# The order of the convolution's parts on TensorE, and a first radial layer of 128 rows, in a two-layer graph network

## The chip, the cores and the metric

The kernel runs on one core of a Trainium2 chip. The metric is the device time of one execution in microseconds, lower is better. A run's time is that of the slowest core, which here is the only one. The core has five engines that run their own instruction queues in order: PE (TensorE, matrix products, with its weight loads shown as PEld), DVE (VectorE), ACT (ScalarE), POOL (GpSimd) and SP (SyncE), and 16 DMA engines. Engines wait for each other by semaphores.

## The reference

There are 6250 nodes with 128 features, and 206,250 directed edges sorted by destination (100,000 random pairs in both directions and one loop per node). Two layers follow each other, each with a residual and a layer norm.

```
# layer 0: attention over incoming edges, then layer norm, a 128-512-128 network, layer norm
m      = leaky_relu(xl[src] + xr[dst] + edge_attr_128 @ W_e)
logits = einsum(m, att);  alpha = softmax over the edges of one dst
out    = segment_sum(xl[src] * alpha, dst)
...
# layer 1: a convolution over incoming edges
h   = gelu(edge_attr_8 @ W_mlp1 / sqrt(8));  h = gelu(h @ W_mlp2 / 8)
w00, w01, w10, w11 = h @ Wp_00, h @ Wp_01, h @ Wp_10, h @ Wp_11
e0, e1 = feat0[src], feat1[src]                 # 32 scalars and 32 vectors of a node
mid0 = concat(w00 * e0 * ea0,  w11 * sum(e1 * ea1))
mid1 = concat(w01 * e0 * ea1,  w10 * e1 * ea0)
n0, n1 = segment_sum(mid0, dst), segment_sum(mid1, dst)
y = cos * self + sin * (n0 @ W2_0e, n1 @ W2_1o)
```

All of it is computed in float32. The node features `feat` that the convolution gathers by source are the output of layer 0, so the convolution's first gather needs the last node of layer 0.

## The kernel before

Edges are cut into tiles of 128, one edge per partition, and into units of 6 tiles (768 edges): 269 units. The class `Fast` runs, in this order, `prologue`, `tables`, `attention` and `convolution`. Rows of a table in DRAM are fetched by source node with one indirect DMA per tile, issued by POOL in `gather` (line 365): 24 in the tables, 1590 in the attention (`xl<-fXL`), and 1614 in the convolution (`f<-fFEAT`).

The convolution, which is where the change lies, goes over 135 pairs of units, each in three parts (`PARTS`) of 2 x 2 tiles. These are its steps for a pair `p` and a part `c`:

- `load(p)` (L766, L768): SP loads the pair's 8 edge scalars, transposed, as a tile `e8` of 16 rows (8 for each unit) by 768, and the 4 edge attributes as `e4`. The pool `ld` gives three buffers for `e8` and four for `e4`.
- `fetch(p)`: POOL issues 12 gathers into a tile `f`, of which there are four.
- `radial(p, k)` (L783, L784): PE multiplies by `m1` (16 x 128) for k = 0 or `m2` (128 x 128, block diagonal) for k = 1, in two halves of 384 columns, and ACT applies the gelu. The result `h1` holds the hidden layer of the two units, 64 rows each.
- `filters(p, c)` (L790): two matmuls give the filter values `w` of four tiles in PSUM. There are three buffers of `w`, one for each part.
- `products(p, c)` (L799, L805, L810, L814): DVE builds a one-hot of the local destination, multiplies it by the edge attributes (`os`), and multiplies `w` by the gathered features (`vy`). There are two buffers each of `os` and `vy`.
- `sums(p, c)` (L831, L833): PE adds up the four tiles by eight matmuls with `vy` as the stationary operand and `os` as the moving one, into `y` in PSUM (two buffers).
- `collect(p)` (L841): DVE adds `y` to the accumulator `acc` at the unit's first destination.
- `nodes.step` runs one further step of `finish`, which takes two finished blocks of 128 nodes through the last product (L889), the layer norm and the store (L901).

In the trace a float32 matmul is two records of PE and two of PEld. The order on each engine is written out by hand (`manual_schedule`) by the loop at the end of `convolution`; the compiler's planner merges the stages where they meet. The indices `p + 2` in that loop are loads, gathers and radials two pairs ahead.

Of the kernel before, what the change touches and what calls it, by code (L numbers as in the profile page):

```python
# [8 lines left out]
F32 = mybir.dt.float32  # L9
# [7 lines left out]
P = 128  # L17
# [18 lines left out]
UE = TU * P  # L36
# [7 lines left out]
HEAD = (3, 4)  # L44
RAW = 4
ENDING = 28


def fast_sizes(n_nodes, n_edges):
# [57 lines left out]
class Fast:  # L107
# [628 lines left out]
    def convolution(self):  # L736


        tc, nc, a, NU = self.tc, self.nc, self.a, self.NU
        NPR, CT = -(-NU // 2), 2  # L740
        PARTS = TU // CT
        with ExitStack() as st:
            def pool(n, b, **k):
                return st.enter_context(tc.tile_pool(name=n, bufs=b, **k))
            cw, ld, wk = pool("fcw", 1), pool("fcl", 3), pool("fck", 2)
# [4 lines left out]
            for x in range(0, self.NX, step):  # L750
                nc.vector.memset(acc[:, :, x:min(x + step, self.NX)], 0.0)
            nodes = Queue(self.finish(st, yp, acc), self.done)
            m1 = cw.tile([16, P], F32, name="m1")
            nc.scalar.dma_start(m1, a["m1"])
            m2 = cw.tile([P, P], F32, name="m2")
            nc.scalar.dma_start(m2, a["m2"])
            wq = cw.tile([P, 2 * D], F32, name="wq")
            nc.scalar.dma_start(wq, a["wq"])
            fs, e8s, e4s, hs, h1s, ws, vys, ys = {}, {}, {}, {}, {}, {}, {}, {}

            def units(p):
                return min(2, NU - 2 * p)

            def load(p):
                e8s[p] = ld.tile([16, UE], F32, name="e8")
                nc.sync.dma_start(e8s[p], a["e8t"][p])  # L766
                e4s[p] = ld.tile([P, 2 * TU, 4], F32, name="e4", bufs=4)
                nc.sync.dma_start(e4s[p], a["e4t"][:, p * 2 * TU:(p + 1) * 2 * TU, :])  # L768

# [5 lines left out]

            def radial(p, k):

                m, x, sc = (m1, e8s, 1.0 / math.sqrt(8.0)) if k == 0 else (m2, h1s, 1.0 / 8.0)
                x = x.pop(p)
                h = (h1s, hs)[k][p] = wk.tile([P, UE], F32, name=f"h{k}")  # L780
                for s in (slice(0, UE // 2), slice(UE // 2, UE)):
                    ps = hp.tile([P, UE // 2], F32, name="h_ps")
                    nc.tensor.matmul(ps, m, x[:, s], start=True, stop=True)  # L783
                    nc.scalar.activation(h[:, s], ps, AF.Gelu_apprx_tanh, scale=sc)  # L784

            def filters(p, c):
                w = ws[p, c] = wp.tile([P, 2 * CT, D], F32, name="w")
                for t in range(CT):
                    e = (c * CT + t) * P
                    nc.tensor.matmul(w[:, 2 * t:2 * t + 2, :], hs[p][:, e:e + P], wq, start=True, stop=True)  # L790
# [29 lines left out]
            def sums(p, c):  # L820


                m = units(p)
                os, vy = vys.pop((p, c))
                if c == 0:
                    ys[p] = yp.tile([P, 2, 4, W], F32, name="y", bufs=2)
                for t in range(CT):
                    for i in range(m):
                        e = 2 * t + i
                        last = c == PARTS - 1 and t == CT - 1 and i == m - 1  # L830
                        nc.tensor.matmul(ys[p][:, i, 0], vy[:, e, 0], os[:, e, 3],  # L831
                                         start=(c == t == i == 0), stop=False)
                        nc.tensor.matmul(ys[p][:, i, 1:], vy[:, e, 1], os[:, e, :3], start=False, stop=last)  # L833

            def collect(p):
                y = ys.pop(p)
                for i in range(units(p)):
                    u = 2 * p + i
                    r = nc.vector.value_load(self.r0[0:1, u:u + 1], min_val=0, max_val=self.n)  # L839
                    v = acc[:, :, bass.ds(r, W)]  # L840
                    nc.vector.tensor_add(v, v, y[:, i])  # L841

            for p in range(min(2, NPR)):
# [1 line left out]
                fetch(p)  # L845
                radial(p, 0)
                radial(p, 1)
            for c in range(PARTS):
                filters(0, c)
            for p in range(NPR + 1):  # L850
                if p + 2 < NPR:
                    load(p + 2)
                    fetch(p + 2)
                for c in range(PARTS):
                    if p < NPR:
                        products(p, c)
                    if p + 1 < NPR:
                        filters(p + 1, c)
                    if c == 1 and p:
                        collect(p - 1)  # L860
                    if p < NPR:
                        sums(p, c)
                    if c != 1 and p + 2 < NPR:
                        radial(p + 2, c // 2)
                    if p:
                        nodes.step(min(2 * p, NU) - 1)
            nodes.rest()


# [548 lines left out]
def _fast_layout(a, g, q):  # L1418
    import numpy as np

    f = np.float32
    n, e = a["x"].shape[0], a["src"].shape[0]
    NU, UP, NP = fast_sizes(n, e)
    EP = NU * UE

    def padded(v, size, fill):
        return np.concatenate([v, np.full((size - len(v),) + v.shape[1:], fill, v.dtype)])

    dst = padded(a["dst"], EP, n)

    more = np.repeat(np.arange(n + 1, n + 1 + UP - NU), UE).astype(dst.dtype)
    dstf = np.concatenate([np.full(1, -1, dst.dtype), dst, more, np.full(1, 2 * n + UP, dst.dtype)])
    x = padded(a["x"], NP, 0)
    ea = padded(a["edge_attr_128"], EP, 0).reshape(NU, UE, D).transpose(0, 2, 1)
    pairs = -(-NU // 2)
    e8 = padded(a["edge_attr_8"], pairs * 2 * UE, 0).reshape(pairs, 2, UE, 8)
    e8 = e8.transpose(0, 1, 3, 2).reshape(pairs, 16, UE)
    e4 = padded(a["edge_attr_4"], pairs * 2 * UE, 0).reshape(pairs, 2, TU, P, 4).transpose(3, 0, 2, 1, 4)
    e4 = e4.reshape(P, -1, 4)[:, :, [1, 2, 3, 0]]

    p = np.arange(P)
    k = np.arange(R8)

    def same(r, c):
        m = np.zeros((P, len(c)), f)
        m[:len(r)] = r[:, None] == c[None]
        return m

    consts = np.concatenate([
        same(p, p),  # L1450
        np.tile(np.arange(W, dtype=f), (P, 1)),
        same(p % W, np.arange(W)),
        same(k % H, p // O),
        same(k + H, k),
        -same(k, k), same(k // H, np.arange(U)),
        same(p, np.arange(H) * O),
        (p % W)[:, None].astype(f)], axis=1)

    u = np.arange(32)
    outer = [u] + [32 + u * 3 + i for i in range(3)]  # L1460
    inner = [c * 32 + u for c in range(4)]
    wfs = np.zeros((D, 2 * D), f)
    w2ab = np.zeros((D, 4, D), f)
    for c in range(4):
        w1 = q["W1_0e"] if c == 0 else q["W1_1o"]
        wfs[np.ix_(outer[c], inner[c])] = w1[:, :32]
        wfs[np.ix_(outer[c], D + outer[c])] = w1[:, 32:]
        w2 = q["W2_0e"] if c == 0 else q["W2_1o"]
        first, second = (w2[:32], w2[32:]) if c == 0 else (w2[32:], w2[:32])
        w2ab[inner[c][:, None], 0, outer[c][None]] = first  # L1470
        for k in (range(1, 4) if c == 0 else [c]):
            w2ab[inner[k if c == 0 else 0][:, None], k, outer[c][None]] = second
    m1 = np.zeros((16, P), f)
    m2 = np.zeros((P, P), f)
    for i in range(2):
        m1[i * 8:i * 8 + 8, i * 64:i * 64 + 64] = q["W_mlp1"]
        m2[i * 64:i * 64 + 64, i * 64:i * 64 + 64] = q["W_mlp2"]
    wq = np.zeros((P, 2 * D), f)
    for i in range(2):
        wq[i * 64:i * 64 + 64, i * D:(i + 1) * D] = np.concatenate(  # L1480
            [q["Wp_00"], q["Wp_01"], q["Wp_10"], q["Wp_11"]], axis=1)
    arrays = {
        "consts": consts,
        "r0": dst[::UE][None],
        "need": np.array(fast_plan(n, e)[2], np.int32)[None],
        "dstf": dstf[None],
        "srct": padded(a["src"], EP, 0).reshape(-1, P).T,
        "dstt": dst.reshape(-1, P).T,
        "x": x,
        "xt": x.T,  # L1490
        "eat": ea,
        "e8t": e8,
        "e4t": e4,
        "w3": np.stack([g["W_l"], g["W_r"], g["W_e"]], axis=1),
        "b_lr": np.concatenate([g["b_l"], g["b_r"]])[None],
        "att": g["att"].reshape(1, -1),
        "rows": np.stack([g[k] for k in ("b_att", "g1", "be1", "b2", "g2", "be2")]),
        "w1": g["W1"],
        "b1": g["b1"].reshape(-1, P).T,
        "w2": g["W2"],  # L1500
        "wfs": wfs,
        "w2ab": w2ab,
        "m1": m1,
        "m2": m2,
        "wq": wq,
    }
    return {k: np.ascontiguousarray(v) for k, v in arrays.items()}
# [105 lines left out]
```

## Time and profile before

| | |
|---|---|
| median of 3 runs | 4443.35 us (4433.61 to 4454.99) |
| profiled execution | 5630.61 us, span 5628.8 us |
| granted TensorE clock, mean of the span | 0.713 |
| attention's gathers (first to last) | 59 to 2673 us |
| first gather of the convolution | 2840.5 us |
| last gather of the convolution | 5564.6 us |
| gathers of the attention / of the convolution | 1590, mean 1067 ns / 1614, mean 955 ns |
| filters L790 | 1620 records, 645.5 us busy |
| sums L831 and L833 | 3228 records each, 667.1 and 918.9 us busy |
| first radial matmuls (16 rows) / second (128 rows) | 540 records, 249.4 us / 540 records, 323.1 us |

A row of the groups gives the line, the engine, the operation, its output and inputs, the count, busy time and mean duration, and then the idle time of the engine just before, with what ended most of it. "issue" is time in which the engine waited for nothing that the profile shows, "remote" is a wait whose releaser isn't told. PEclk is the granted TensorE clock, as a part of full speed. Rows of the order in time start with the start and the duration in microseconds; idle time before is in brackets.

### The profile page before, as it was taken

Reading aid. Unit: us, or ns where it says so; the run is one execution under the profiler, and the core shown is the slowest. Engines: PE = TensorE matmul, PEld = TensorE weight load, DVE = VectorE, ACT = ScalarE, POOL = GpSimd, SP = SyncE. Lnnn points to the kernel's source line nnn. Section 1 sums busy time; section 2 is a strip of 40 time slices with the busy share of each in tenths; the row PEclk is TensorE's granted clock in tenths of the full one; section 3 lists DMA queues with packets and bytes.
Section 4 is the critical chain, followed back from the end, with each engine's and each line's share of the span. In section 5 each row is a group of like instructions: output and inputs, shape, how many; then the busy total and the mean of one; then the engine's idle time right before and its main releaser. Section 6 shows DMA issues by size and latency. Waiting matters only on the chain. (4 is left out here: it accounts for less than half of the span.)

```text
span 5628.8 us, 67318 instructions
## 1 busy us (share of the span) xinstructions
PE 4052.6 (72%) x21381; PEld 3207.9 (57%) x21381; DVE 2536.3 (45%) x5657; ACT 947.9 (17%) x2530; POOL 3262.0 (58%) x3232
## 2 busy tenths in 40 slices
PE   3666666676666676665648778788887888778878
PEld 2454555555545555544536666676666666667656
DVE  1455655655655665554713333333333333333333
ACT  1111222222221222211311111111111111111111
POOL 6256666766766766765045555555555555555553
PEclk6577777777777777767756766676767766666766
DMA  4443444444443444433111111111111111111111
GB/s 117 133 111 108 113 108 111 116 108 112 112 113 107 117 112 111 109 103 99 35 40 44 45 47 43 44 46 47 47 46 45 47 47 45 47 41 47 44 43 28
DMA packets 292393, 427.71 MB, mean 76 GB/s; under 512 B 124589, under 2 KB 201359, under 8 KB 292031
## 3 DMA queue, kind: packets, MB, share of 16 engines
q0 software_dynamic: 103296, 218.27, 16.0%
q1 hardware_dynamic: 185146, 197.75, 11.7%
q10 hardware_dynamic: 3588, 7.31, 0.4%
q8 instruction: 174, 2.85, 0.2%
q14 instruction: 189, 1.54, 0.1%
HBM read 403.04 MB, written 19.96 MB: 75 GB/s over the span
## 5 line engine op out<-in xcount | busy, mean ns | idle before, releaser
L365 POOL DMA_INDIRECT f<-fFEAT,fsrc x1614 | 1542.0, 955 | 1349.3 <-DVE oh L799 597.0
L365 POOL DMA_INDIRECT xl<-fXL,fsrc x1590 | 1696.9, 1067 | 934.5 <-issue 429.2
L790 PE MATMUL w<-wq,h 128*128 128x256 f32 x1620 | 645.5, 539 | 470.3 <-DVE vy L814 259.4
L805 DVE TENSOR_TENSOR os<-oh,e 128x512 f32<-128x512 f32 x405 | 280.6, 693 | 1490.4 <-remote 581.9
L833 PE MATMUL y<-os,vy 128*128 128x96 f32 x3228 | 918.9, 375 | 34.5 <-issue 34.4
L790 PEld LDWEIGHTS w<-wq,h 128*128 128x128 f32 x1620 | 396.0, 265 | 717.8 <-issue 395.7
L419 PE MATMUL z<-fw,ea 128*128 128x136 f32 x3228 | 654.8, 347 | 142.1 <-DVE pr L438 66.4
L831 PEld LDWEIGHTS y<-os,vy 128*128 128x128 f32 x3228 | 714.7, 258 | 73.0 <-issue 23.3
L833 PEld LDWEIGHTS y<-os,vy 128*128 128x128 f32 x3228 | 670.4, 256 | 35.6 <-issue 35.5
L831 PE MATMUL y<-os,vy 128*128 128x32 f32 x3228 | 667.1, 293 | 28.0 <-issue 26.6
L419 PEld LDWEIGHTS z<-fw,ea 128*128 128x128 f32 x3228 | 554.6, 242 | 208.0 <-issue 106.4
L784 ACT ACTIVATE h<-h_ps 128x384 f32<-128x384 f32 x540 | 252.8, 489 | 2418.5 <-remote 823.9
L528 PE MATMUL m<-xl,oh 128*32 128x136 f32 x3228 | 247.5, 348 | 239.6 <-ACT s L511 92.7
L814 DVE TENSOR_TENSOR vy<-w,f 128x384 f32<-128x384 f32 (+1 forms) x810 | 408.0, 545 | 0.0
L541 PEld LDWEIGHTS m<-fcst,sb 128*128 128x128 f32 x1076 | 191.2, 234 | 359.0 <-ACT sb L533 199.5
L541 PE MATMUL m<-fcst,sb 128*128 128x32 f32 x1076 | 180.3, 299 | 228.6 <-ACT sb L533 166.8
L783 PE MATMUL h_ps<-h,m 128*128 128x384 f32 x540 | 323.1, 738 | 23.5 <-issue 22.9
L422 PE MATMUL z<-xl,fcst 128*128 128x408 f32 x538 | 310.9, 660 | 15.4 <-issue 15.0
L528 PEld LDWEIGHTS m<-xl,oh 128*32 128x32 f32 x3228 | 128.7, 126 | 297.5 <-ACT s L511 95.1
L444 DVE TENSOR_REDUCE lg<-pr 128x48 f32<-128x816 f32 x269 | 266.8, 992 | 1.6 <-DVE pr L438 1.6
L519 DVE TENSOR_TENSOR xl<-xl,ex 128x768 f32<-128x768 f32 x269 | 255.3, 949 | 15.6 <-ACT ex L504 15.6
L419 PE MATMUL z<-xr,oht 96*128 96x136 bf16 x1614 | 227.5, 254 | 39.8 <-issue 34.2
(143 smaller groups left out, 4130.3 us busy)
## 6 DMA issues: line engine op xcount, KB each, us to landing
ea<-fast_eat_dram SPq DMA_DIRECT2D x269, 384.0 KB
lb<-fLB SPq DMA_DIRECT2D x269, 144.0 KB
f<-fFEAT,fsrc POOLq DMA_INDIRECT x1614
xl<-fXL,fsrc POOLq DMA_INDIRECT x1590
xr<-fXR SPq DMA_DIRECT2D x807, 8.5 KB
e<-fast_e8t_dram SPq DMA_DIRECT2D x135, 48.0 KB
fXR<-pt SPq DMA_DIRECT2D x16, 306.0 KB
fXL<-tb SPq DMA_DIRECT2D x16, 204.0 KB
```

What stands on the lines that cost most here:

```text
L365: self.nc.gpsimd.indirect_dma_start(out=to, out_offset=None, in_=table, in_offset=bass.IndirectOffsetOnAxis(ap=self.src[:, g:g + 1], axis=0))
L419: nc.tensor.matmul(z[:, t * ZW:(t + 1) * ZW], lhs[:, e], rhs, start=(t == 0 and lhs is ea), stop=(half == 1 and t == 2 and lhs is oht))
L422: nc.tensor.matmul(z, self.ident, xl[:, :3, :].rearrange("p t f -> p (t f)"), start=False, stop=True)
L444: nc.vector.tensor_reduce(lgs[b][:, :, i * H:(i + 1) * H], prs.pop(u).rearrange("p (t h) o -> p t h o", h=H), axis=mybir.AxisListType.X, o ...
L528: nc.tensor.matmul(ag[q * W:(q + 1) * W], oh[:, t, :], xl[:, t, :], start=(t < 4), stop=(t + 4 >= TU))
L541: nc.tensor.matmul(nd[:, i, j], sb[:, j], self.s4, start=True, stop=True)
L783: nc.tensor.matmul(ps, m, x[:, s], start=True, stop=True)
L790: nc.tensor.matmul(w[:, 2 * t:2 * t + 2, :], hs[p][:, e:e + P], wq, start=True, stop=True)
L805: nc.vector.tensor_mul(os[:, own], oh.rearrange("p t u w -> p (t u) w")[:, own, None, :].to_broadcast([P, n, 4, W]), e4s[p][:, at, :, None ...
L814: nc.vector.tensor_mul(vy[:, own, j, 32:].rearrange("p t (c x) -> p t c x", c=3), w[:, :, None, 64 + j * 32:96 + j * 32].to_broadcast([P, ...
L831: nc.tensor.matmul(ys[p][:, i, 0], vy[:, e, 0], os[:, e, 3], start=(c == t == i == 0), stop=False)
L833: nc.tensor.matmul(ys[p][:, i, 1:], vy[:, e, 1], os[:, e, :3], start=False, stop=last)
```

## The change

Three things are changed, all in `convolution` and the arrays that it loads.

The loop runs over parts `q = 3 p + c` instead of pairs and parts. At part `q` it issues products(q), then collect of the pair before (at c = 1), then sums of part q - 1, then filters of part q + 2, then the radial (at c = 0 and 2), then the step of the nodes. Before, a part was products(q), filters(q + 3), collect, sums(q), radial, nodes. Ahead of the loop there are now two filters instead of three.

The first radial layer works on 128 rows: one tile `e8` holds eight pairs one below the other (16 rows each), loaded at once, with two buffers. `m1` becomes eight matrices of 128 x 128, of which matrix k has the weights in rows 16 k to 16 k + 15 and zeros elsewhere, so that the product picks out pair k of the eight. The last group has seven pairs and 112 rows.

The constant `EB = 8` is that number of pairs.

```diff
-            m1 = cw.tile([16, P], F32, name="m1")
+            m1 = cw.tile([P, EB, P], F32, name="m1")
             nc.scalar.dma_start(m1, a["m1"])
...
             def load(p):
-                e8s[p] = ld.tile([16, UE], F32, name="e8")
-                nc.sync.dma_start(e8s[p], a["e8t"][p])
+                if p % EB == 0:
+                    g = min(EB, NPR - p)
+                    e8 = ld.tile([P, UE], F32, name="e8", bufs=2)
+                    nc.sync.dma_start(e8[:g * 16], a["e8t"][p:p + g].rearrange("g k e -> (g k) e"))
+                    for i in range(g):
+                        e8s[p + i] = e8[:g * 16], m1[:g * 16, i]
...
-                m, x, sc = (m1, e8s, 1.0 / math.sqrt(8.0)) if k == 0 else (m2, h1s, 1.0 / 8.0)
-                x = x.pop(p)
+                if k == 0:
+                    (x, m), sc = e8s.pop(p), 1.0 / math.sqrt(8.0)
+                else:
+                    x, m, sc = h1s.pop(p), m2, 1.0 / 8.0
...
-            for c in range(PARTS):
-                filters(0, c)
-            for p in range(NPR + 1):
-                if p + 2 < NPR:
+            for q in range(2):
+                filters(q // PARTS, q % PARTS)
+
+            for q in range(NQ + PARTS):
+                p, c = q // PARTS, q % PARTS
+                if c == 0 and p + 2 < NPR:
                     load(p + 2)
                     fetch(p + 2)
-                for c in range(PARTS):
-                    if p < NPR:
-                        products(p, c)
-                    if p + 1 < NPR:
-                        filters(p + 1, c)
-                    if c == 1 and p:
-                        collect(p - 1)
-                    if p < NPR:
-                        sums(p, c)
-                    if c != 1 and p + 2 < NPR:
-                        radial(p + 2, c // 2)
-                    if p:
-                        nodes.step(min(2 * p, NU) - 1)
+                if q < NQ:
+                    products(p, c)
+                if c == 1 and p:
+                    collect(p - 1)
+                if 0 < q <= NQ:
+                    sums((q - 1) // PARTS, (q - 1) % PARTS)
+                if q + 2 < NQ:
+                    filters((q + 2) // PARTS, (q + 2) % PARTS)
+                if c != 1 and p + 2 < NPR:
+                    radial(p + 2, c // 2)
+                if p:
+                    nodes.step(min(2 * p, NU) - 1)
...
-    m1 = np.zeros((16, P), f)
+    m1 = np.zeros((P, EB, P), f)
...
+        for k in range(EB):
+            m1[k * 16 + i * 8:k * 16 + i * 8 + 8, k, i * 64:i * 64 + 64] = q["W_mlp1"]
```

## The prediction

> **What bounds the kernel now.** I read the page first (busy times, slices), then the groups by line, the waits of the last stage, and PE and POOL in order of time with busy times by stretch.
>
> ```profile
> span 5628.8 us, 67318 instructions
> PE 4052.6 (72%) x21381; PEld 3207.9 (57%) x21381; DVE 2536.3 (45%) x5657; ACT 947.9 (17%) x2530; POOL 3262.0 (58%) x3232
> POOL 6256666766766766765045555555555555555553
> PEclk6577777777777777767756766676767766666766
> ...
> L365 POOL DMA_INDIRECT f<-fFEAT,fsrc x1614 | 1542.0, 955 | 1349.3 <-DVE oh L799 597.0
> L365 POOL DMA_INDIRECT xl<-fXL,fsrc x1590 | 1696.9, 1067 | 934.5 <-issue 429.2
> ```
>
> No engine is full, TensorE's clock is granted at 0.7, and POOL, which only gathers rows, has idle time that DVE ends. Taken alone this page says: PE and DVE hold each other up, POOL has room. But the page is of an execution of 5630.61 us (1.8 us around its span), and the median of the runs is 4443.35, 21% less. The extra must sit somewhere. PE in order of time, at the start of the convolution, shows where:
>
> ```profile
> 2882.26 0.21 PE L831 MATMUL y<-os,vy 128*128 128x32 f32 x1 [1.88 <-issue]
> 2885.06 0.32 PE L833 MATMUL y<-os,vy 128*128 128x96 f32 x1 [2.59 <-issue]
> 2887.86 0.32 PE L833 MATMUL y<-os,vy 128*128 128x96 f32 x1 [2.48 <-issue]
> ```
>
> One small matmul every 2.8 us, waiting for nothing that is shown; elsewhere a whole part's sixteen such records take 1.75 (3671.45 to 3673.20). Such stretches recur. I take them to belong to the profiled execution (inferred: only something of this size explains the 21%). POOL keeps its pace in the same stretch:
>
> ```profile
> 2840.54 0.94 POOL L365 DMA_INDIRECT f<-fFEAT,fsrc  x1 [166.28 <-DMA fBASE<-h]
> 2841.79 0.94 POOL L365 DMA_INDIRECT f<-fFEAT,fsrc  x1 [0.30 <-issue]
> ```
>
> 1.249 us from gather to gather (0.94 + 0.30) wherever nothing blocks it. So for the median I build the time from POOL. Head until the first xl gather 59; attention 1590 x (1.067 + 0.30) = 2174; pause until the first f gather, 167 in the profile, of which I estimate 40 to be PE's backlog and stalls: 127; convolution 1614 x 1.249 = 2016; tail after the last gather, 63 profiled, some 25 to 30 when PE is not two pairs behind. Sum 4401 to 4406. With everything as profiled it is 59 + 2174 + 167 + 2016 + 63 = 4479, with undisturbed gathers in attention (1590 x 1.249 = 1986) and the short pause and tail 4213. The measured 4443 lies inside, so gathers alone nearly fill the median: some 40 us are left over, for both stages (0 to 230 by the ends).
>
> Now the convolution per pair of units. POOL: 12 x 1.249 = 15.0 us. DVE, from the groups: 3 x (0.28 + 0.69 + 0.42 + 2 x 0.55) + 2 x 0.28 = 8.0. PE depends on its clock:
>
> ```profile
> core 0: us, PE busy (x) PEld busy (x) DVE busy (x) ACT busy (x) POOL busy (x), PEclk, DMA share, GB/s
> 3602.00:3609.00 7.00, 7.00 (x23) 5.04 (x22) 2.15 (x5) 0.78 (x2) 0.92 (x1) 0.50 0.02 4
> 3630.00:3638.00 8.00, 8.00 (x32) 7.28 (x32) 2.15 (x5) 0.14 (x1) 5.97 (x6) 0.51 0.20 55
> 3666.00:3680.00 14.00, 12.95 (x84) 10.84 (x84) 8.02 (x23) 1.49 (x4) 7.98 (x8) 1.00 0.14 39
> 3000.00:5500.00 2500.00, 2028.56 (x8709) 1640.95 (x8710) 888.01 (x2256) 315.32 (x606) 1403.69 (x1471) 0.70 0.17 45
> ```
>
> PE is busy without a gap at clock 0.50 in the first two rows, at 1.00 in the third. In order of time, a pair at full clock runs from 3666.18 to 3679.12, less 1.82 of output matmuls (L889): 11.1 us. At half clock its pieces are filters 1.87, sums 3.36, radial 2.85 (16 rows) and 2.57: 3 x 5.23 + 5.42 = 21.1. PE keeps up with POOL's 15.0 if it does over (21.1 - 15.0) / 10.0 = 61% of its work at full clock.
>
> **The Trainium skill.** "TensorE: Matmul & The Clock Gate", Part 1, says that the clock is halved or full by how busy PE was in windows of about 3.4 us. The trace agrees on 0.50 and 1.00, and adds that full occupancy doesn't suffice: the first two rows hold a first radial layer (16 rows) or mostly weight loads with small matmuls, and stay at half; the clock rises at the ends of pairs, around the second layer (128 rows). The same page, "LDWEIGHTS", says that a load costs by columns, not rows; shortest records here are 181 (16 rows) against 186 ns (128), and 481 against 486 for the matmuls: agrees. "Perfetto Trace Analysis", "DMA Instruction — SWDGE (GPSIMD)", says the record of such a DMA ends when its descriptors are made: so 0.94 us is POOL's own work, which the 1.249 pace bears out, and no faster consumer shortens it.
>
> **The change part by part.**
> (1) Order on PE. Before, a step is filters(q+3), sums(q), radial; the filters wait until products(q) has read the buffer, and the first filters of a pair follow at once on the radial that feeds them, through ACT:
>
> ```profile
> PE w L790 <- DVE vy L814: 216.7, 68, 10.7
> PE w L790 <- ACT h L784: 100.8, 11, 14.1
> ```
>
> Together 317.5 over the window 3200 to 5400, about 106 pairs (2200 us at 2789 / 135): 3.0 us a pair, most of it in waits of 4 to 14 us that I count to the profiled execution. A clean one (3664.29 to 3666.18) is 1.9. After, sums(q-1) come first, filters(q+2) need a buffer that products(q-1) left, and the radial is two parts old. Gain for PE 0.5 to 2 us a pair (I take 1), worth 0 where POOL sets the pace. No instruction is added. New wait: radial and filters stand behind sums(q-1), hence behind products(q-1); DVE's products(q+1) wait for these sums, as they did. Collect(p-1) now stands one part behind the last sums it needs: not late.
> (2) 128 rows. Matmul and load time unchanged (5 ns a record). The stationary matrix is zero outside its pair, so results stay. If rows count as activity, the 2.85 us of radial and the filters before it make a busy window, and the share at full clock rises: from 0.70 to, I guess, 0.85 to 0.95, 2 to 4 us a pair for PE. Bound from below: rows don't count, 0.
> (3) Loads. 135 e issues of 48 KB on SP become 17 of 384 KB; an issue takes 0.42 us on SP, so 118 x 0.42 = 50 us of SP's time, hidden: SP mostly waits for DVE (e4's buffers). A group is issued about two pairs (30 us) ahead; by the fit in "DMA: Bandwidth & Descriptors", "Anatomy of one DMA — SWDGE (gpsimd) path" (2.0 us + bytes / 436 GB/s, made for another queue, so an estimate) it lands in 2.9. m1 grows from 8 to 512 KB: 3.2 instead of 1.8 us as the trace has it. PE has the first radials ahead of the last node group's transposes, but these wait until 2811 for ACT anyway, and the filters end at 2793.5: 18 us cover it; without cover it costs 1.4.
> (4) Gathers: same 1614, same buffers (4 pairs), same order.
>
> Sum: PE's pair falls by 1 + 3 = 4 us, from 11.1 / 0.7 = 15.9 (less where the clock is better than in the profile) to 11.1 / 0.9 = 12.3, and POOL's 15.0 stays. The gain is what PE costs above 15.0 now, which the 40 us left over bound: 0.3 us a pair if all is in the convolution. I take a quarter to a third, as attention has slow stretches of its own: about 13 us, **4430 us**.
>
> **Rivals.**
> (A) Gathers bind, above: 4415 to 4450. For: the sum and POOL's steady pace. Against: POOL's 597 us behind DVE, if they are no artefact.
> (B) PE falls behind by more than the two pairs of f buffers in part of the convolution, so that POOL waits: then most of the excess there is returned, 0.2 to 0.8 us x 135 = 30 to 110: centre 4385. For: half clock with a busy PE.
> (C) Unprofiled gathers are quicker, say 1.10 (13.2 us a pair), and PE binds at 11.1 / 0.7 = 15.9 or so: after, 13.2 to 14.4; 1.5 to 2.7 x 135 = 200 to 360, about 4230. For: a granted clock of 0.70 leaves PE little room. Against: gathers then fill only 59 + 1590 x 1.22 + 127 + 1775 + 28 = 3929 of 4443, so attention would hold 150 to 300 us of waits; and no gather in the trace starts sooner than 1.245 after the last.
> (D) Slower: the big m1 lands late at the head of the convolution. PE takes its queue in order, so the last node group waits behind the radials, then FEAT, then the first gather. It decides from 18 us late; above 0.5% it needs 18 + 22 = 40 late against an estimate of 1.4: 4470. Little speaks for it; its chance stands also for buffer placement and order that the compiler sets at this boundary, where DVE's eight memsets (8 x 2.69 = 21.5 us) lie between node steps and may fall worse, or better.
>
> **Numbers.** A 0.40, B 0.27, C 0.18, D 0.15. Two runs of this kernel differ by up to 0.5%, so that is the bound of no change (4421 to 4466). Faster B + C = 0.45; same A 0.40; slower 0.15. The range runs from 4250 (half of C left out, 0.09) to 4468 (0.08 above); A alone has 4415 to 4450.
>
> **What would show it.** Right: f gathers again 1.25 us apart and the time moved under 25 us, while in the profile the granted clock of the convolution rises to 0.8 or more, and filters no longer wait for vy or h. The profiled span may fall much more than the median, since there PE's side binds. Part (2) is wrong if a window with the 128-row first layer still doesn't raise the clock; (1) if filters still show DVE's or ACT's waits. The prediction falls if the median drops by over 60 us with the gather pace unchanged (B), or if f gathers take less time than 1.249 each (C).

## The result, and the profile after

| | before | after |
|---|---|---|
| median, on one chip | 4450.22 us (4433.61 to 4457.10, 10 runs) | 4467.53 us (4457.17 to 4473.93, 10 runs) |
| ratio | | 1.0043, 95% interval 1.0028 to 1.0058 |

The changed kernel is slower: 17 us between the medians, 0.43% by the ratio. That is within the 0.5% that the prediction called no change and at the upper end of its range (4468), but the forecast was a gain, to 4430, and the measured time lies 38 us above it. The page of after:

```profile
span 4454.9 us, 66591 instructions
PE 3553.6 (80%) x21381; PEld 2921.3 (66%) x21381; DVE 2558.1 (57%) x5657; ACT 963.1 (22%) x2528; POOL 3325.7 (75%) x3232
POOL 6777777777777777777715777777777777777776
PEclk8878877878777877788768888888888888888888
...
L366 POOL DMA_INDIRECT xl<-fXL,fsrc x1590 | 1723.5, 1084 | 486.9 <-issue 402.8
L366 POOL DMA_INDIRECT f<-fFEAT,fsrc x1614 | 1579.2, 978 | 603.9 <-issue 444.6
```

This profiled execution took about what the runs take, so it can't be set against the 5628.8 us shown for before. The kernel before was therefore profiled again (experiment 1); this execution has no stretches of 2.8 us per small matmul, so those belonged to the one execution, as the prediction had inferred. Its page:

```profile
span 4432.0 us, 67318 instructions
PE 3633.7 (82%) x21381; PEld 2922.6 (66%) x21381; DVE 2552.7 (58%) x5657; ACT 966.4 (22%) x2530; POOL 3306.9 (75%) x3232
POOL 6777777777777777777725777777777777777776
PEclk7887778778787777788777887878778787888878
...
L365 POOL DMA_INDIRECT xl<-fXL,fsrc x1590 | 1714.8, 1079 | 487.7 <-issue 408.2
L365 POOL DMA_INDIRECT f<-fFEAT,fsrc x1614 | 1569.0, 972 | 601.5 <-issue 440.1
```

Set side by side, the two pages show this. PE is busy 80 us less and its clock rose, as the change promised. The "<-DVE oh" that had ended POOL's idle time in the disturbed page is gone from both, and POOL is never idle for more than 0.32 us between two gathers of a stage. POOL sets the pace in both kernels. And the f gathers, the one thing that I had costed at nothing, are 6 ns longer in the mean (978 against 972), in 1614 of them 10 us.

From the starts and ends of the gathers the span splits like this (us; "f stage" is from the start of the first f gather to the end of the last, "attention" the same for xl, "pause" what lies between):

| | head | attention | pause | f stage | tail |
|---|---|---|---|---|---|
| before (experiments 1 and 9) | 45.4, 44.9 | 2199.2, 2203.3 | 109.9, 116.4 | 2060.6, 2061.1 | 16.8, 17.4 |
| after, and again (experiment 7) | 44.7, 44.6 | 2207.8, 2211.0 | 112.3, 115.0 | 2070.7, 2073.5 | 19.3, 18.7 |

The f stage is 11.2 us longer (2072.1 against 2060.9) and the tail 1.9. Attention, whose code is the same in all the kernels below, varied from 2195.1 to 2211.7 with no tie to the kernel: mean 2204.0 over eleven profiled executions with the new order, 2204.5 over eight with the old. So its 8 us here are no effect of the change. The pause averages 115.0 with the new order (nine executions that clear `acc` on DVE), 114.4 with the old (seven); by the other parts of the change, it is 114.8 with the bigger `m1` and the grouped loads (ten), 114.7 without (six). The f stage and the tail make 13 of the 17 us, and the interval of the ratio reaches from 12.5 to 25.8 us. The tail's part is not certain: in other executions it is as short as 17.2 with the new order (experiment 2) and as long as 19.3 with the old (experiment 3).

What PE and DVE wait for inside the f stage (waits over 2370 to 4430 us: engine, line, releaser, us in total, times, longest). The kernel before, undisturbed:

```profile
PE w L790 <- DVE vy L814: 163.3, 65, 4.5
...
DVE os L805 <- PE y L833: 500.7, 233, 6.1
DVE vy L810 <- DMA f<-fFEAT,fsrc: 267.8, 112, 6.2
```

After:

```profile
PE y L840 <- DVE vy L823: 257.2, 86, 5.2
...
DVE vy L819 <- DMA f<-fFEAT,fsrc: 840.8, 193, 12.2
DVE os L814 <- PE y L842: 155.7, 92, 3.0
```

The filters no longer wait for DVE; in their place the sums do, 257 us in all, so PE's wait for DVE has moved and not shrunk. DVE's wait for PE fell from 501 to 156 us. DVE spends the time gained waiting for gathered rows, 841 instead of 268 us. The change put the filters out of DVE's reach as it says; DVE is now tied to the gathers instead of to PE. Why that makes gathers longer is seen in order of time. DVE in after (start, duration):

```profile
3008.47 0.43 DVE L819 TENSOR_TENSOR vy<-w,f 128x256 f32<-128x256 f32 x1 [0.17 <-DMA f<-fFEAT,fsrc]
...
3009.74 0.70 DVE L850 TENSOR_TENSOR acc<-acc,y 128x128 f32 x2
3010.36 0.29 DVE L808 TENSOR_TENSOR oh<-fl,fcst 128x128 f32<-128x128 f32 x1
3010.74 0.69 DVE L814 TENSOR_TENSOR os<-oh,e 128x512 f32<-128x512 f32 x1
3011.36 0.42 DVE L819 TENSOR_TENSOR vy<-w,f 128x256 f32<-128x256 f32 x1
...
3012.99 0.69 DVE L814 TENSOR_TENSOR os<-oh,e 128x512 f32<-128x512 f32 x1
```

POOL at the same time:

```profile
3008.32 0.94 POOL L366 DMA_INDIRECT f<-fFEAT,fsrc  x1 [0.30 <-issue]
3009.56 0.94 POOL L366 DMA_INDIRECT f<-fFEAT,fsrc  x1 [0.30 <-DVE vy L823]
3010.81 1.45 POOL L366 DMA_INDIRECT f<-fFEAT,fsrc  x1 [0.30 <-issue]
3012.56 0.94 POOL L366 DMA_INDIRECT f<-fFEAT,fsrc  x1 [0.30 <-issue]
```

The os product that runs from 3010.74 to 3011.43 lies over the start of the gather at 3010.81, and this gather takes 1.45 us instead of 0.94. The os at 3012.99 starts 0.43 us into a gather, and that gather keeps its 0.94. Over all 1614 f gathers the time above 0.943 each adds up to 47.0 and 47.6 us in the two executions of before, to 57.2 and 59.9 in those of after: 11 us more, which is the whole difference of the f stages.

### The profile page after: what moved, and what is told of

Its sections match the earlier page's. It is cut to its first block, busy times and chain, and to the rows that moved or that the text cites. A ratio compares the mean times of both kernels' runs of the same rounds, so it can differ in the third digit from the quotient of the medians.

```text
span 4454.9 us, 66591 instructions
## 1 busy us (share of the span) xinstructions
PE 3553.6 (80%) x21381; PEld 2921.3 (66%) x21381; DVE 2558.1 (57%) x5657; ACT 963.1 (22%) x2528; POOL 3325.7 (75%) x3232
## 5 line engine op out<-in xcount | busy, mean ns | idle before, releaser
L366 POOL DMA_INDIRECT f<-fFEAT,fsrc x1614 | 1579.2, 978 | 603.9 <-issue 444.6
L840 PEld LDWEIGHTS y<-os,vy 128*128 128x128 f32 x3228 | 610.5, 226 | 376.4 <-DVE vy L823 313.4
L842 PE MATMUL y<-os,vy 128*128 128x96 f32 x3228 | 831.5, 345 | 3.9
L840 PE MATMUL y<-os,vy 128*128 128x32 f32 x3228 | 611.9, 275 | 260.9 <-DVE vy L823 260.9
L819 DVE TENSOR_TENSOR vy<-w,f 128x256 f32<-128x256 f32 x405 | 170.3, 420 | 848.4 <-DMA f<-fFEAT,fsrc 843.8
L842 PEld LDWEIGHTS y<-os,vy 128*128 128x128 f32 x3228 | 589.4, 228 | 12.2 <-DVE vy L823 11.7
L799 PE MATMUL w<-wq,h 128*128 128x256 f32 x1620 | 535.2, 463 | 0.0
L423 PEld LDWEIGHTS z<-xl,fcst 128*128 128x128 f32 x538 | 101.0, 234 | 414.4 <-issue 347.3
L799 PEld LDWEIGHTS w<-wq,h 128*128 128x128 f32 x1620 | 340.5, 233 | 36.4
L436 DVE TENSOR_TENSOR pr<-z,xl 128x408 f32<-128x408 f32 x269 | 154.9, 576 | 209.8 <-DMA xl<-fXL,fsrc 100.3
L426 ACT ACTIVATE pr<-z 128x24 f32<-128x24 f32 x269 | 56.9, 211 | 820.7 <-PE z L423 419.6
```

Source lines behind the costliest of these rows:

```text
L366: self.nc.gpsimd.indirect_dma_start(out=to, out_offset=None, in_=table, in_offset=bass.IndirectOffsetOnAxis(ap=self.src[:, g:g + 1], axis=0))
L423: nc.tensor.matmul(z, self.ident, xl[:, :3, :].rearrange("p t f -> p (t f)"), start=False, stop=True)
L840: nc.tensor.matmul(ys[p][:, i, 0], vy[:, e, 0], os[:, e, 3], start=(c == t == i == 0), stop=False)
```

## The experiments

Two theories stood against each other. The **collision theory** (theory C in the first expectations): a gather is lengthened when an os product runs at its start, and the new order puts more of them there. The **boundary theory** (theory B): what differs lies ahead of the first f gather, where the bigger `m1`, the grouped loads and the clearing of `acc` meet the last node group. (These letters are not those of the prediction's cases.) Ratios are to the kernel before on the same chip. The last two columns count the f gathers whose start fell inside an os product, and their mean duration (in the first execution of after they are 228 and 1.187 us, with 0.978 for all); the mean of all other f gathers is 0.944 to 0.947 us in every row.

| experiment | ratio, 95% interval | f stage us | f gathers mean us | under os | their mean us |
|---|---|---|---|---|---|
| 1 before | 0.9998 (0.9988 to 1.0008) | 2060.6 | 0.972 | 233 | 1.135 |
| 2 order alone | 1.0018 (1.0009 to 1.0026) | 2068.3 | 0.977 | 215 | 1.193 |
| 3 128 rows and grouped loads alone | 0.9986 (0.9976 to 0.9997) | 2052.2 | 0.967 | 178 | 1.146 |
| 4 after, collect in the third part | 0.9976 (0.9967 to 0.9985) | 2051.8 | 0.967 | 184 | 1.141 |
| 5 before without os | 0.9905 (0.9889 to 0.9921) | 2015.3 | 0.944 | - | - |
| 6 after without os | 0.9900 (0.9882 to 0.9917) | 2014.8 | 0.944 | - | - |
| 7 after again | 1.0040 (1.0026 to 1.0054) | 2073.5 | 0.980 | 208 | 1.226 |
| 8 after, collect in DVE's wait, 3 os buffers | 0.9948 (0.9933 to 0.9964) | 2040.6 | 0.960 | 113 | 1.174 |
| 9 before again | 0.9996 (0.9986 to 1.0007) | 2061.1 | 0.973 | 234 | 1.135 |
| 10 after, 3 os buffers | 1.0048 (1.0033 to 1.0063) | 2077.7 | 0.983 | 186 | 1.281 |
| 11 before, acc cleared on POOL | 0.9962 (0.9947 to 0.9977) | 2064.1 | 0.974 | 246 | 1.138 |
| 12 as 8, acc cleared on POOL | 0.9906 (0.9890 to 0.9922) | 2040.1 | 0.959 | 123 | 1.150 |
| 13 before, oh in PSUM, one h_ps | 1.1203 (1.1177 to 1.1228) | 2539.0 | 0.944 | 161 | 0.943 |
| 14 after, oh in PSUM, one h_ps | 0.9915 (0.9897 to 0.9933) | 2019.3 | 0.946 | 223 | 0.946 |
| 15 after, one h_ps | 1.0023 (1.0014 to 1.0032) | 2069.2 | 0.977 | 185 | 1.214 |
| 16 all together | 0.9859 (0.9837 to 0.9881) | 2015.4 | 0.944 | 95 | 0.943 |
| 17 before, one h_ps | 1.1188 (1.1162 to 1.1213) | 2538.7 | 0.966 | 184 | 1.134 |
| 18 as 3, one h_ps | 0.9974 (0.9964 to 0.9984) | 2040.2 | 0.960 | 128 | 1.128 |

**1 to 4: which part of the change costs.** Experiment 1 is the kernel before, unaltered. Experiment 2 has the new loop with the 16-row layer and single loads, experiment 3 the other two parts in the old loop.

> The kernel before, unchanged, for a profile without the stretches in which TensorE crawled, and as the measure of what two equal kernels differ by. Theory C (collisions): POOL gathers back to back here too; the convolution's gathers take a mean of about 0.968 us against 0.978 after the change (17 us / 1614), because the vector engine's os product falls less often on a gather's start; the pause between the stages is 112 us within 3. Theory B (boundary): the gathers have the same mean, 0.978, and the pause is some 17 us shorter, about 95. Time: 1.000 of before within 0.2%.

> The new loop order alone, with the first radial layer of 16 rows and one load of e8 per pair. Theory C: 1.004 of before, with 0.975 to 0.980 us per gather in the convolution and the pause as before, since the order sets when os starts. Theory B: 1.000 of before, as the big m1 and the grouped e8 are not there.

> The first radial layer of 128 rows with the grouped loads alone, in the old loop order. Theory C: 1.000 of before, gathers at about 0.968 us. Theory B: 1.004 of before, the whole 17 us in the pause between the stages. Either way TensorE's clock in the convolution is higher than in the kernel before, if rows count as activity: 0.8 or more against 0.7 or less.

The order costs 0.18%, less than the 0.4% that theory C expected of it and more than the nothing of theory B; its f stage is 7.4 us longer than in the two executions of before, with the mean gather (0.977) where theory C had it. The 128 rows with the grouped loads gain 0.14%, with the f stage 8.7 us shorter. So the loss is the order's, and the two parts don't add: together they lose 0.43%. The boundary theory, which put the loss on `m1` and the loads, has it in the wrong part. Experiment 4 moves the two additions of collect, 0.70 us of DVE, by one part (and lets the step of the nodes that reads the accumulator follow them):

```diff
-                if c == 1 and p:
+                if c == 2 and p:
                     collect(p - 1)
...
-                    nodes.step(min(2 * p, NU) - 1)
+                    nodes.step(min(2 * p, NU) - 1 if c == 2 else 2 * p - 3)
```

> The changed kernel with collect (0.7 us of the vector engine) behind the third part's products instead of the second's, so that the third os starts 0.7 us earlier, in the middle of a gather and not at the next one's start (the step of finish that reads the accumulator waits one part longer). Theory C: the long gathers fall from 162 to 110 or fewer, 20 us less than the changed kernel: 0.999 of before. Theory B: as the changed kernel, 1.004.

Moving 0.7 us of DVE work, on an engine that is 57% busy, moved the time from 1.0043 to 0.9976, past the kernel before. No work was taken away: what counts is when DVE does it. The gain is larger than the expected 0.999.

**5 and 6: os products left out.** The product is formed for the first two parts and read again in all later ones, so 403 of the 405 os products are left out, and with them the sums' right values.

```diff
+                if 3 * p + c < 2:
+                    oss.append(cw.tile([P, 2 * CT, 4, W], F32, name=f"os{c}"))
...
+                os = oss[(3 * p + c) % 2]
-                os = wk.tile([P, 2 * CT, 4, W], F32, name="os")
```

> The kernel before, with the product os of one-hot and attributes formed for the first two parts only and read again for all later ones: 403 DVE products of 128x512 (0.69 us each) are left out, so the output is wrong; all gathers, filters, sums and the other DVE products stay. Collision theory: gathers lengthen when an os product starts just before or at their start; without them the mean f gather falls from 0.972 to 0.945-0.952, the f stage from 2061 to 2018-2030, the time by 30 to 43 us, ratio to before 0.990-0.993. Boundary theory (what differs between the kernels lies in the pause before the first f gather): gathers stay at 0.97, ratio 0.998-1.002.

> The changed kernel with the same omission (os formed for the first two parts only; the output is wrong). Collision theory: the f stage falls from 2071 to the same 2018-2030 as in the kernel before without os, so 40 to 53 us are saved against the changed kernel, and the two kernels without os lie within 0.2% of each other, ratio to before 0.989-0.994. Boundary theory: still 15-20 us slower than the kernel before without os, about 1.003 to before.

Both f stages fall to 2015, 1614 times 1.249, and 0.5 us apart; the difference between the two orders is gone. So the os products cost the f stage 46 us in the kernel before and 57 in the changed one. Leaving them out also takes work from DVE; experiments 4, 8 and 14, which keep that work, tell the two apart.

**7 and 9: the same kernels again.**

> The changed kernel, unaltered, beside the others on one chip. Both theories: ratio to before 1.003-1.006. Collision theory: the f stage in its trace again 2065-2075, with the pause at 110-118. Boundary theory: f stage as in the kernel before, 2052-2061, and a pause or attention stage that is longer by 15.

> The kernel before, unaltered, for the spread of its stages from execution to execution. Collision theory: an f stage of 2053-2064 again (clearly under the 2071 and 2074 of the changed kernel), attention's stage anywhere in 2197-2212, as it has been for either kernel. Rival (the phase between os and the gathers is chance, not set by the order of the code): an f stage anywhere in 2050-2075.

The f stage of either kernel repeats within 3 us, and so does where its os products fall. The third os of a pair starts 0.95 us or more after the start of a gather, so at its end or in the gap ahead of the next, in 104 and 111 of 135 pairs after, and in 53 and 42 before; with the order alone (experiment 2) in 109, with the 128 rows in the old order (experiment 3) in 50. The phase isn't chance: the order sets it.

**8 and 10: collect where DVE waits anyway.** In the listing above, vy starts 0.15 us after a gather, when its rows have landed; vy, collect and oh take 2.27 us to the next os, which is two paces of 1.25 less 0.23: the os begins just ahead of the next gather. Without collect it is 1.63 us (3011.36 to 3012.99), which from the same start would be 0.15 + 1.63 - 1.25 = 0.53 us into a gather. Experiment 8 puts collect between os and vy of the first part, and gives os a third buffer; `values` is the vy half of `products`, set apart for that. Experiment 10 has the buffer alone.

```diff
-                os = wk.tile([P, 2 * CT, 4, W], F32, name="os")
+                os = wk.tile([P, 2 * CT, 4, W], F32, name="os", bufs=3)
...
-                if c == 1 and p:
-                    collect(p - 1)
                 if 0 < q <= NQ:
                     sums((q - 1) // PARTS, (q - 1) % PARTS)
+                if c == 0 and p:
+                    collect(p - 1)
+                if q < NQ:
+                    values(p, c)
```

> The changed kernel with the two DVE additions of collect moved from the second part of a pair to the first, between its os and its vy, where DVE waits some 8 us for the last six gathers of the pair, and with three os buffers instead of two, so that os no longer waits for PE: os then follows at a fixed time (about 1.66 us) after vy, and vy starts about 0.1 us after a gather's start, so that os starts 0.5 us after one. Same instructions and same work. Collision theory: few os start within 0.3 us of a gather's start, the mean f gather falls to 0.948-0.96, the f stage to 2023-2045, the time to 0.990-0.996 of before (25 to 48 us less than the changed kernel). Boundary theory: as the changed kernel, 1.003-1.005.

> The changed kernel with a third os buffer alone: os no longer waits for the sums of two parts before, so PE no longer sets when it starts; collect stays in the second part. If PE's wait is what puts os on the starts of gathers: f stage 2030-2050, ratio to before 0.994-0.999. If it is the place of collect (0.6 us of DVE work between vy and the next os): f stage 2060-2075, ratio 1.001-1.005.

DVE in experiment 8, in order of time:

```profile
3014.57 0.69 DVE L813 TENSOR_TENSOR os<-oh,e 128x512 f32<-128x512 f32 x1
```

and POOL:

```profile
3014.20 0.94 POOL L366 DMA_INDIRECT f<-fFEAT,fsrc  x1 [0.30 <-issue]
3015.45 0.95 POOL L366 DMA_INDIRECT f<-fFEAT,fsrc  x1 [0.30 <-issue]
```

The os starts 0.37 us into a gather and is done before the next. The third os now falls late in 10 of 135 pairs, and the f stage is 32 us shorter than after. The third buffer alone does not help (2077.7, some 6 us more than after): os then follows vy and collect more strictly, late in 112 pairs, so PE's wait was not what put it there; the place of collect is, as experiment 4 says too. The 61 os products that still fall late in experiment 8 (21 in first parts, 30 in second, 10 in third) lengthen the gathers that follow by 21 us, most of the 26 that experiment 8 still has above the 2015 of experiments 5 and 6.

**13 to 16: which property of os does it.** Lengthening by os has a sharp form. In after, by how long the os still runs past the start of the gather (us):

| os ends after the start by | 0 to 0.1 | 0.1 to 0.2 | 0.2 to 0.3 | 0.3 to 0.4 | 0.4 to 0.5 | 0.5 to 0.6 | 0.6 to 0.7 | over 0.7 |
|---|---|---|---|---|---|---|---|---|
| gathers | 32 | 9 | 14 | 7 | 34 | 68 | 24 | 40 |
| gather longer than 0.943 by, mean | 0.00 | 0.03 | 0.11 | 0.22 | 0.33 | 0.43 | 0.50 | 0.00 |

The gather loses the whole overlap but some 0.12 us: each of the lengthened ones ends 0.81 to 0.83 us after the os, wherever it began. It is held up, not slowed. The 40 gathers of the last column start within 0.05 us of the os and keep their time, and there it is the os that takes longer, 0.72 to 0.77 us instead of 0.69. So one of the two waits for the other, and never both. One such os and its gather in after:

```profile
3054.48 0.75 DVE L814 TENSOR_TENSOR os<-oh,e 128x512 f32<-128x512 f32 x1
```

```profile
3054.50 0.94 POOL L366 DMA_INDIRECT f<-fFEAT,fsrc  x1 [0.30 <-issue]
```

It isn't enough that DVE works: 397 other gathers start under a vy of 128x384, and take 0.944 in the mean and 0.954 at most.

The Trainium skill, "SBUF — State Buffer", section "Who interferes with whom", says that a DVE instruction with two SBUF inputs contends with a GpSimd instruction that reads SBUF, and that this contention is an exclusive lock, so that one waits for the other. os has both inputs in SBUF, and the gather reads its list of rows (`fsrc`) there; vy, with `w` in PSUM, has one. The same section also says that tensor_tensor, the operation of os, had not stalled a DMA in an earlier probe; here it does, from 0.944 to up to 1.467 us, so for these gathers the measurement decides.

To try the rule of two SBUF inputs, `oh` was put into PSUM; for the room, `h_ps` has one buffer instead of two, for which experiment 15 is the control. The instructions, their sizes and their order stay.

```diff
-            hp, wp, yp = pool("fhp", 2, space=PSUM), pool("fwp", PARTS, space=PSUM), pool("fyp", 1, space=PSUM)
+            hp, wp, yp = pool("fhp", 1, space=PSUM), pool("fwp", PARTS, space=PSUM), pool("fyp", 1, space=PSUM)
...
-                oh = wk.tile([P, CT, 2, W], F32, name="oh")
+                oh = yp.tile([P, CT, 2, W], F32, name="oh")
```

> The kernel before with the one-hot oh in PSUM instead of SBUF (and, for its room, one h_ps buffer instead of two): os still runs, as long and as often, but reads only one input from SBUF. If the two SBUF inputs of os hold the gathers up: gathers at 0.943-0.947, f stage 2015-2022, ratio 0.989-0.993, as without os (0.9905). If any DVE work at a gather's start does: f gathers stay at 0.965-0.98, ratio 0.998-1.005.

> The changed kernel with the one-hot in PSUM and one h_ps buffer. Two SBUF inputs: f stage 2015-2022, ratio to before 0.988-0.993, level with e13 within 0.2%. Any DVE work: f stage 2065-2080, ratio 1.002-1.006.

> Control: the changed kernel with one h_ps buffer instead of two and nothing else. PE waits for ACT between the halves of a radial layer (some 0.8 us, four times a pair at most), hidden behind the gathers: f stage 2060-2080, ratio to before 1.001-1.006 by either theory.

> The changed kernel with the one-hot in PSUM (one h_ps buffer), collect in the wait of the first part, three os buffers, and acc cleared by POOL. Two SBUF inputs: f stage 2015-2022 and pause 85-97, ratio to before 0.983-0.988. Any DVE work: as e12, 0.989-0.992.

Experiment 14, DVE and then POOL in order of time:

```profile
3009.76 0.69 DVE L814 TENSOR_TENSOR os<-oh,e 128x512 f32<-128x512 f32 x1
```

```profile
3009.91 0.95 POOL L366 DMA_INDIRECT f<-fFEAT,fsrc  x1 [0.30 <-issue]
```

The same overlap as in after (os from 0.15 us ahead of the gather to 0.54 past its start), and the gather keeps its time. Of 223 gathers under an os the longest takes 0.957 us. os itself takes 0.69 in every one of its 402 full products; the longer ones are gone too. `oh`, whose two inputs stay in SBUF, still lengthens the 46 gathers that start under it, to 0.965 in the mean. So it is the second SBUF input, and not DVE's work as such: the trace agrees with the rule of two SBUF inputs. That the list of rows is what the gather reads then is an inference. With os out of the way the changed kernel takes 0.9915 of before; the control has 1.0023, and the kernel is some 1.1% faster than the control.

The attention, which all these kernels leave as it is, shows the same in one trace. Its line 439 runs one DVE operation of 128x384 twice, once on `pr` in SBUF, once on `z` in PSUM, each with the table `fattb` in SBUF. In after:

```profile
1085.63 0.56 DVE L439 SCALAR_TENSOR_TENSOR pr<-pr,fattb 128x384 f32<-128x384 f32 x1
1421.23 0.54 DVE L439 SCALAR_TENSOR_TENSOR pr<-z,fattb 128x384 f32<-128x384 f32 x1
```

```profile
1085.72 1.28 POOL L366 DMA_INDIRECT xl<-fXL,fsrc  x1 [0.30 <-issue]
1421.33 0.94 POOL L366 DMA_INDIRECT xl<-fXL,fsrc  x1 [0.30 <-issue]
```

The 160 gathers that start under the first kind take 1.133 us in the mean, the 73 under the second 0.943. All of attention's gathers together are 224 us above 0.943 each, four times what the f stage loses and 5% of the kernel. How much of it can be won was not tried.

**13, 17, 18: what the change does for PE.** The kernel before with the one-hot in PSUM had gathers of 0.944, as expected, and was 12% slower, as neither theory expected. Two controls tell why.

> Control for e13: the kernel before with one h_ps buffer and nothing else. If the buffer makes PE bind in the kernel before (PE at half clock after each 16-row layer): f stage 2500-2600, POOL gaps of 400 us or more, clock in the convolution 0.62-0.70, ratio 1.11-1.14. If the one-hot in PSUM was what cost e13: f stage 2050-2070, ratio 0.998-1.005.

> 128 rows and grouped loads alone, in the old order, with one h_ps buffer. If the clock that 128 rows bring is what keeps PE ahead: clock 0.8 or more, no POOL gaps, f stage 2045-2075, ratio 0.995-1.005. If the new order is needed: POOL gaps of 200 us or more, ratio 1.05-1.13.

One h_ps buffer alone costs the kernel before 11.9%; the one-hot has no part in it. Experiment 17, busy times from 2500 to 4300 us, and POOL's waits in the f stage:

```profile
2500.00:4300.00 1800.00, 1686.87 (x6594) 1317.92 (x6593) 667.19 (x1695) 241.81 (x451) 1093.33 (x1131) 0.64 0.17 48
```

```profile
POOL f L365 <- DVE oh L799: 419.5, 87, 9.7
```

Experiment 18, the same stretch with the 128-row layer in the old order:

```profile
2500.00:4300.00 1800.00, 1568.10 (x8437) 1252.27 (x8436) 867.39 (x2174) 311.86 (x581) 1366.57 (x1423) 0.87 0.21 61
```

Clock 0.64 against 0.87 with the same waits between the halves of a layer, POOL 420 us behind DVE's oh (DVE itself stands behind PE, 1240 us in all for os over the whole execution) against none. PE in experiment 17, in order of time, shows the first layer of 16 rows at work:

```profile
3014.10 0.91 PE L783 MATMUL h_ps<-e,m 16*128 16x384 f32 x2
3015.59 1.57 PE L783 MATMUL h_ps<-e,m 16*128 16x384 f32 x2 [0.58 <-ACT h L784]
3017.09 2.08 PE L790 MATMUL w<-wq,h 128*128 128x256 f32 x4
```

In this pair the clock falls to half within the layer: its second half takes 1.57 instead of 0.91, and the filters that follow 2.08, where they take 1.03 at their quickest in the same trace. So the 128 rows, with the grouped loads that come with them, are worth 12% where PE sets the pace (1.1188 against 0.9974), and next to nothing where POOL does (0.9986, experiment 3). Rows and loads were not tried apart; that it is the rows rests on the clock.

**11 and 12: the boundary has a price, but no part in the change.** In the chain of after the eight clearings of `acc` stand between steps of the last node group:

```profile
2306.51 0.71 issue
2307.22 2.69 DVE acc L752
```

```diff
-                nc.vector.memset(acc[:, :, x:min(x + step, self.NX)], 0.0)
+                nc.gpsimd.memset(acc[:, :, x:min(x + step, self.NX)], 0.0)
```

> The kernel before, with the eight clearings of acc done by POOL, which is idle there, instead of DVE, where they stand between the steps of the last node group (8 x 2.69 us, each with 0.6 us of issue before it in the chain that ended last). If that boundary work sets the start of the first f gather: the pause falls from 110-118 to 85-97, ratio 0.994-0.996. If something else does: 0.999-1.001. The f stage stays at 2053-2064.

> The changed kernel with collect in the wait of the first part and three os buffers, and with acc cleared by POOL. If the two gains are independent they add: pause 85-97, f stage 2035-2045, ratio 0.989-0.992, the fastest complete kernel. If the clearing on POOL is late or delays the first gather: 0.994-0.997.

POOL in experiment 12:

```profile
2300.16 21.39 POOL L752 MEMSET acc<- 128x3152 f32 x8 [51.54 <-PE n L667]
```

POOL clears as fast as DVE, in a pause of its own that it would have idled through. The pause falls from 110.6 (experiment 8) to 87.6, and from 116.4 (experiment 9) to 102.6; the second fall is smaller than the one to 85 to 97 that I expected. The gains add: experiment 12 takes 0.9906, and experiment 16, with the one-hot in PSUM as well, 0.9859 (4378.41 us median, 66 us below that of before on the same chip): the fastest of the complete kernels.

## Why the prediction was wrong

- **What bounds the kernel: right.** The sum over POOL's gathers holds with other terms: head 45 (59), attention 2199 to 2203 (2174), pause 110 to 116 (127), f stage 2061 (2016), tail 17 (25 to 30). That the sum came within 40 us of the median was in part luck: attention and f stage were put some 72 us too low, head, pause and tail some 38 too high, and the "40 us left over" are what these errors leave. The reading of the 2.8 us matmuls as a matter of one execution was right.
- **The "40 us left over": the step that failed.** I gave part of it to PE and took "a quarter to a third" as the gain. In the f stage PE cost nothing: POOL has no gap there. The 45 us between 2061 and 2016 were gathers held up, by os nearly all of them. The pace of 1.249 that I called the pace "wherever nothing blocks it" was never asked what blocks it; the mean of 955 ns in the page against 0.94 for an undisturbed gather said that something did, 20 us of that execution. Likewise for "no faster consumer shortens it": what could lengthen a gather was not asked, though attention's 1.067 stood beside the 0.94.
- **Part (4), "Gathers: same 1614, same buffers (4 pairs), same order", put at nothing: the step that turned the sign.** A gather's time depends on what DVE runs at its start. The change adds 11 us there, against a price of 0, and that is most of the 17 us measured. I had asked of each wait who waits behind it, and not where the freed engine would put its work.
- **Part (1): right that the filters stop waiting and that PE's gain is worth 0 where POOL binds.** The filters' wait for vy (163 us) is gone, and DVE's wait for PE fell by 345 us. The new wait that it named, behind products(q-1), is there as well: 257 us at the sums. A gain for PE of 1 us a pair is not shown.
- **Part (2): right in sign, too large in size.** Clock of the stretch 2500 to 4300: 0.81 before, 0.85 after, at the low end of the guess of 0.85 to 0.95; 0.64 against 0.87 where PE binds. The start was better than the 0.70 that I took from the disturbed execution, so there was less to gain: with the 128 rows alone PE is busy 108 us less in that stretch (experiment 3 against 1), by my estimate 0.9 us for each of its some 118 pairs, not 2 to 4.
- **Part (3): right.** Pause 114.8 with the bigger `m1` and the grouped loads against 114.7 without; nothing of them shows.
- **The rivals.** A comes nearest (gathers bind), but it had only no gain. B and C fall: POOL waits for nothing in the f stage. D had the right sign and the wrong place: the clearings of `acc` do cost something, 7 to 14 us of pause in the kernel before and 23 in the changed one as experiment 8 has it, but the change has no part in it.

Open: why the 128 rows in the old order have fewer gathers under an os (178) than the kernel before (233). That they do is measured; which wait moved them was not tried. Nor is it known why the new order costs more with the 128 rows (0.43%) than without them (0.18%).

## What to carry to other kernels

When one engine's back-to-back work sets the time, its durations are not constants: compare the mean of its records with the shortest, and find what runs beside the long ones before pricing a change at nothing. A change that relieves an engine off the critical path moves that engine's work in time, and here the worth of moving 0.7 us of DVE work by one part was 0.7% of the kernel (experiment 4). If GpSimd gathers set the pace, keep DVE instructions with two SBUF inputs off their starts, or put one input into PSUM; and look at every stage, for here the stage that the change left alone loses four times as much.

## What was unexpected of the hardware

- An indirect gather of 128 rows (0.944 us, every 1.249) that starts 0.05 us or more after a DVE product of 128x512 with two SBUF inputs, and 0.1 us or more before its end, ends some 0.82 us after that product: it takes up to 1.47 us. If the two start within 0.05 us of each other, the gather keeps its time and the product takes up to 0.77 instead of 0.69. With one input in PSUM, no effect on either (223 overlaps in experiment 14).
- A product that starts 0.35 to 0.65 us into a gather is harmless: of 157 gathers in after none takes more than 0.95 us.
- Clearing 128x3152 floats takes POOL 21.4 us for eight, DVE 8 x 2.69 = 21.5 us.
- With the 16-row layer one PSUM buffer less costs 12%, at a granted clock of 0.64; with 128 rows and grouped loads it costs nothing, at 0.87 (experiments 17 and 18).
